# Other work dealt to the pairs of a scan by a budget of PE time, with a cap on ScalarE's parts between exps

## The chip, the cores and the metric

The kernel runs on one core of one Trainium2 chip. The metric is the time of the whole program on the device in microseconds; the time before is the median of three runs. A core has TensorE (PE in the profile), VectorE (DVE), ScalarE (ACT), GpSimd (POOL) and SyncE (SP), which here only issues the transfers. Each engine works through its own instructions in order, and semaphores tie the engines together.

## The reference: what is computed

The input is 8 sequences of 1024 tokens with 512 features, f32. It is normalized, and two branches read the result; the output is their sum with the input:

```python
xn = _layernorm(x)
x = x + mamba(xn, ...) + ffn(xn, w_gate, w_up, w_down)
```

The first branch is a Mamba block with 1024 inner channels and 16 states for each of them:

```python
x_branch, z = split(xn @ W_in)
xc = silu(causal_conv4(x_branch) + conv_b)
ssm = xc @ W_x                       # B (16), C (16) and one step value per token
dt = softplus(ssm[..., -1:] + dt_bias)
h = h * exp(dt * A) + (dt * xc) * B  # for every token in turn
y = (sum over states of h * C + xc * D_param) * silu(z)
out = y @ W_out
```

The second is a gated feed-forward layer of width 1408 in which inputs, weights and the hidden values are rounded to FP4 with one scale for each 16 values:

```python
h = silu(q(xn) @ q(w_gate).T) * (q(xn) @ q(w_up).T)
ffn = q(h) @ q(w_down).T
```

## The kernel before, in words

**Chunks and pairs.** The 8192 tokens are 16 chunks of 512. The scan over tokens is done for 128 rows at once, a row being one channel and one state: 32 channels by 4 states. A chunk has 8 channel blocks of 128 (j), 4 groups of states (q) and, for each, 4 sets of 32 channels that are worked on two at a time (h). So a chunk is 8 x 4 x 2 = 64 **pairs**, the whole kernel 1024. A pair is, in order of its dependencies: `make_u` (POOL, L471) multiplies dt*x by B; `make_a` (ScalarE, L480) makes two exps of 128x512 into PSUM; `scan` (DVE) runs two scans (L491), keeps the last state (L497) and multiplies by C (L499) into one of four `hc` buffers. Every second pair, `sum_states` (PE, L510) adds the states up into `py`. u is made two pairs ahead (three buffers), the exps one pair ahead (two PSUM buffers).

**Two sweeps.** `run` first prepares: weights and inputs are quantized, transposed and written to HBM, and the first chunk is projected. Then `sweep` goes over pairs 0 to 639 (chunks 0 to 9), and again over pairs 640 to 1023 (chunks 10 to 15). Each sweep spreads other work over its pairs:

- `finish` (L547), the output projection of the chunk before, in pairs 2 to 9 of a chunk (`END_Y`, `QUIET`).
- `ahead` (L447), the projections of the next chunk: for each of 8 blocks two halves of x (PE L331, then on ScalarE and DVE the convolution, L338 and L343), and z (PE L354, copied on ScalarE L361). Then `silus`, `parameters` (L381) and `steps_of` (softplus on ScalarE, L427). It runs from pair 9 on and is to be done by pair 43.
- in the first sweep `gate_up` (L564): 96 pieces, one for each chunk and 256 columns of the hidden width. A piece is four groups of matmuls (L589; gate for two pairs of token tiles, then up for the same), silu on ScalarE (L600), a multiply on DVE (L604), the scales on DVE (L613 to L619), five quantizing operations on POOL and ScalarE (L623 to L627, L55, L56), and `put`, which transposes on PE (L639), copies on ScalarE (L642) and stores.
- in the second sweep `downs` (L688): for each of 64 token tiles 11 matmuls (L705), whose sum `add` (L537) adds to the residual.

All are generators that yield the PE time (us) of the part that they have just issued. The order is written out by this planner, and the scheduler keeps it. At each pair, `sweep` issues the pair, then `issue` issues what has come due, and then takes parts from the generators. `later(n, work)` puts what follows a matmul (an evacuation, say) n pairs later. Gate/up's rate is its whole cost divided by the number of pairs that it may use, whatever else PE is given in that pair:

```python
slots = len(now) * (per - QUIET + END_Y) / per - TAIL
...
while spent < cost * passed / slots and self.room("other") and not self.hold:
```

**Banks.** Three PSUM banks serve all these matmuls. `bank` takes the next; `room` says whether the third last one has had the instruction issued that reads it out.

**Queues.** All transfers in the sweeps are issued by SP, in order. Projection weights (`weights`, L319) have two buffers; x's for the next block are asked for after the second half of x, z's at the block's start. The residual tile `r` (L543) is asked for after the matmuls that are added to it.

Of the kernel before, what the change touches and what calls it, by code (L numbers as in the profile page):

```python
# [17 lines left out]
P = 128  # L18
# [3 lines left out]
DOWN = 1.0 - 2.0**-23  # L22
STEEP = 0.47 * math.log(2.0)
# [10 lines left out]
QUIET = 9  # L34
TAIL = 12
# [47 lines left out]
class Net:  # L83
# [185 lines left out]
    def later(self, n, work, bank=None):  # L269

        self.due.setdefault(self.now + n, []).append((work, bank))
        if not self.timed:
            self.issue()

    def issue(self):
        while self.due.get(self.now):
            work, bank = self.due[self.now].pop(0)
            work()
            if bank is not None:
                bank[1] = False  # L280
        self.due.pop(self.now, None)
        if not self.timed and self.due:
            self.now = min(self.due)
            self.issue()
# [34 lines left out]
    def weights(self, s, j, off, name):  # L319
        w = self.pool.tile([P, self.KM, P], F32, tag="w", name=f"w{name}_{s.c}_{j}")  # L320
        self.nc.sync.dma_start(w, self.Win_v[:, :, off + j * P : off + (j + 1) * P])
        return w

    def project_x(self, s, j, i, w):
# [22 lines left out]
        self.later(1, convolve, b)  # L347

    def project_z(self, s, j, w):
# [13 lines left out]
        self.later(1, copy, b)  # L363

    def silus(self, s, h):
# [13 lines left out]
        self.later(1, store)  # L379

    def parameters(self, s):  # L381
# [24 lines left out]
        self.later(1, store, b)  # L406
        self.later(2, row)
        for h in range(self.J // 2):
            self.later(4 + 2 * h, lambda h=h: self.steps_of(s, h))
# [11 lines left out]
    def steps_of(self, s, h):  # L421
# [15 lines left out]
        self.later(1, rest)  # L437
# [99 lines left out]
    def add(self, t, b):  # L537
# [4 lines left out]
        r = self.pool.tile([P, self.DM], F32, tag="r", name=f"r_{t}_{seen}")  # L542
        nc.sync.dma_start(r, self.r_d[t] if seen else self.x[tok, :])  # L543
        self.later(1, lambda: nc.vector.tensor_tensor(r, r, b[0], ALU.add), b)
        self.later(2, lambda: nc.sync.dma_start(self.out[tok, :] if seen else self.r_d[t], r))

    def finish(self, s):  # L547
        nc = self.nc
        for i in range(self.TT):
            t = s.c * self.TT + i  # L550
            b = self.bank([P, self.DM], f"po_{t}")
# [7 lines left out]
            self.add(t, b)  # L559
# [4 lines left out]
    def gate_up(self, fp, chunks):  # L564
# [5 lines left out]
        full = []  # L570
# [35 lines left out]
        def scales(c, n, h, pu):  # L606
# [311 lines left out]
```

## Time and profile before

| what | value |
|---|---|
| median of 3 runs (lowest, highest) | 5607.41 us (5598.88, 5613.46) |
| the profiled execution, time and span | 5612.34 us, 5610.6 us |
| granted clock of PE over the span | 0.907 |
| first scan; first scan of the second sweep | 529.9 us; 3871.2 us |
| mean time of a pair, first and second sweep | 5.22 us, 4.44 us |
| two scans, one product with C | 2 x 1.227 to 1.287 us, 1.221 us |
| two exps; one u | 2 x 0.691 us; 2.360 us |

Durations are means of groups of the profiled execution. Busy time is what an engine spends on instructions of its own; waits and issues of transfers are not in it. A wait is written as the engine with the instruction that waited, an arrow, what released it, then the sum in us, the number of times and the longest. A busy PE is not a PE at its peak, since its clock can be granted in part (PEclk).

### The profile page before, as it was taken

How to read it: one execution, taken by the hardware profiler on the slowest of the kernel's cores; microseconds unless marked ns; L12 is line 12 of the kernel's file. 1: busy time of each engine (PE TensorE's matmuls, PEld its weight loads, DVE VectorE, ACT ScalarE, POOL GpSimd, SP SyncE). 2: the span in 40 equal slices, each digit the busy share in tenths (PEclk: the TensorE clock that was granted, in tenths of full speed). 3: DMA queues.
4: the chain of work that ended last, by engine and by line, in shares of the span. 5: the costliest groups of instructions: out<-in, count | busy, mean ns of one | idle time of the engine just before them, and what ended most of it. 6: DMA issues, size and time to landing. Idle time of an engine off the chain costs nothing.

```text
span 5610.6 us, 55655 instructions
## 1 busy us (share of the span) xinstructions
PE 4593.5 (82%) x17604; PEld 2572.4 (46%) x17604; DVE 4954.0 (88%) x5958; ACT 3022.8 (54%) x4042; POOL 3576.4 (64%) x1706
## 2 busy tenths in 40 slices
PE   4533888988898898988888798886989898989886
PEld 3322555645555465555555555552424242424221
DVE  5676889898988989999898898988999999999997
ACT  4664565655656566565655656554444444444432
POOL 6565676686766768676765867666465646465654
PEclk8755999989999998999999998997999999999997
DMA  6565565565665657566565655656676767676752
GB/s 175 156 184 152 136 172 153 160 193 147 180 161 152 166 154 188 151 184 167 159 174 154 182 153 166 168 153 178 171 198 176 196 174 196 176 198 172 194 144 69
DMA packets 635574, 937.75 MB, mean 167 GB/s; under 512 B 58624, under 2 KB 378112, under 8 KB 635152
## 3 DMA queue, kind: packets, MB, share of 16 engines
q1 hardware_dynamic: 624880, 931.66, 60.3%
q10 hardware_dynamic: 10400, 2.52, 0.2%
q8 instruction: 141, 2.31, 0.2%
q14 instruction: 153, 1.25, 0.1%
HBM read 676.81 MB, written 257.20 MB: 166 GB/s over the span
## 4 chain that ended last, share of the span: by engine, by line
DVE 42%; PE 24%; ACT 12%; issue 8%; DMA 7%; POOL 5%; SPq 1%; ACTq 0%; DVEq 0%; POOLq 0%
DVE ah L491 24%; DVE hc L499 7%; PE pu L589 4%; PE pz L354 4%; PE px L331 3%; ACT ah L480 3%; PE po L553 3%; DVE xc L343 3%; PE pod L705 3%; PE pg L589 2%; PE py L510 2%; DVE pu L613 2%; DMA rep<-ddd 1%; ACT L480 1%; DVE h L604 1%
## 5 line engine op out<-in xcount | busy, mean ns | idle before, releaser
L471 POOL TENSOR_TENSOR u<-rep,B 128x1024 f32<-128x1024 f32 x1024 | 2416.5, 2360 | 1504.7 <-DVE ah L491 1425.4
L480 ACT ACTIVATE ah<-rep,A 128x512 f32<-128x512 f32 x2048 | 1414.0, 691 | 1866.0 <-DVE hc L499 1818.4
L491 DVE TENSOR_TENSOR_SCAN ah<-ah,state,u 128x512 f32<-128x512 f32 x1024 | 1318.1, 1287 | 53.4 <-ACT ah L480 34.5
L491 DVE TENSOR_TENSOR_SCAN ah<-ah,u 128x512 f32<-128x512 f32 x1024 | 1256.7, 1227 | 89.5 <-ACT ah L480 67.7
L499 DVE TENSOR_TENSOR hc<-ah,C 128x1024 f32<-128x1024 f32 x1024 | 1250.0, 1221 | 56.7 <-PE py L510 16.5
L510 PE MATMUL py<-hc,summed 128*32 128x512 f32 x4096 | 713.8, 640 | 248.3 <-DVE hc L499 248.1
L589 PE MATMUL pu<-wu,xq 128*128 128x256 f32 (+1 forms) x3072 | 698.0, 385 | 62.8 <-ACT h L600 19.2
L589 PE MATMUL pg<-wg,xq 128*128 128x256 f32 (+1 forms) x3072 | 658.8, 370 | 45.5 <-DMA xq<-xqT 15.5
L705 PE MATMUL pod<-dT,hTr 128*128 128x512 f32 x1408 | 669.2, 624 | 14.9 <-DMA hTr<-hT 10.2
L589 PEld LDWEIGHTS pu<-wu,xq 128*128 128x128 f32 x3072 | 579.8, 205 | 194.6 <-ACT hT L642 25.7
L589 PEld LDWEIGHTS pg<-wg,xq 128*128 128x128 f32 x3072 | 548.7, 194 | 196.5 <-issue 78.0
L331 PE MATMUL px<-xT,wx 128*128 128x259 f32 x2048 | 547.9, 417 | 104.1 <-issue 24.1
L331 PEld LDWEIGHTS px<-xT,wx 128*128 128x128 f32 x2048 | 407.7, 206 | 284.9 <-issue 93.9
L354 PE MATMUL pz<-xT,wz 128*128 128x512 f32 x1024 | 479.7, 612 | 27.6 <-ACT ah L480 12.8
L343 DVE SCALAR_TENSOR_TENSOR xc<-px,cw,xc 128x256 f32<-128x256 f32 x768 | 369.6, 481 | 115.6 <-ACT xc L338 98.2
L553 PE MATMUL po<-Wout,y 128*128 128x512 f32 x1024 | 462.4, 603 | 1.2 <-DVE y L531 1.2
L705 PEld LDWEIGHTS pod<-dT,hTr 128*128 128x128 f32 x1408 | 272.6, 200 | 412.9 <-issue 391.6
L510 PEld LDWEIGHTS py<-hc,summed 128*32 128x32 f32 x4096 | 100.6, 111 | 669.8 <-DVE hc L499 404.0
L354 PEld LDWEIGHTS pz<-xT,wz 128*128 128x128 f32 x1024 | 193.5, 194 | 270.1 <-issue 207.4
L553 PEld LDWEIGHTS po<-Wout,y 128*128 128x128 f32 x1024 | 190.9, 191 | 267.7 <-issue 262.5
L623 POOL TENSOR_TENSOR qv<-h,rs 128x1024 f32<-128x1024 f32 x96 | 171.6, 1788 | 221.4 <-DVE rs L619 202.3
L480 ACT ACT_TABLE_LOAD x201 | 257.9, 1283 | 3.6
(108 smaller groups left out, 4182.9 us busy)
## 6 DMA issues: line engine op xcount, KB each, us to landing
rep<-ddd SPq DMA_DIRECT2D x512, 512.0 KB, 7.3
ddd<-dd SPq DMA_DIRECT2D x128, 512.0 KB, 3.2
hTr<-hT SPq DMA_DIRECT2D x64, 704.0 KB, 6.9
wg<-gu SPq DMA_DIRECT2D x80, 512.0 KB, 6.5
wu<-gu SPq DMA_DIRECT2D x80, 512.0 KB, 5.2
hT<-hT SPq DMA_DIRECT2D x80, 512.0 KB, 5.5
wx<-in_L_attn_W_in_dram SPq DMA_DIRECT2D x128, 256.0 KB, 3.5
wz<-in_L_attn_W_in_dram SPq DMA_DIRECT2D x128, 256.0 KB, 3.6
```

The costliest lines, as they stand in the source:

```text
L331: nc.tensor.matmul(px[:, : H0 + TH], w[:, k, :], s.xT[:, k, i * TH : i * TH + H0 + TH], start=(k == 0), stop=(k == self.KM - 1),)
L343: nc.vector.scalar_tensor_tensor(ca, px[:, k : k + TH], self.cw[:, j, k : k + 1], ca, ALU.mult, ALU.add)
L354: nc.tensor.matmul(b[0], w[:, k, :], s.xT[:, k, self.H0 :], start=(k == 0), stop=(k == self.KM - 1))
L471: self.nc.gpsimd.tensor_tensor(u, s.reps[j][:, h : h + 2, 1, :], s.B[q].unsqueeze(1).to_broadcast([P, 2, T]), ALU.mult)
L480: self.nc.scalar.activation(ah[:, i, :], s.reps[j][:, h + i, 0, :], AF.Exp, scale=self.A[:, g, q : q + 1])
L491: nc.vector.tensor_tensor_scan(ah[:, i, :], ah[:, i, :], u[:, i, :], 0.0 if s.first else self.state[:, g + i, q : q + 1], ALU.mult, ALU.add,)
L499: nc.vector.tensor_tensor(hc, ah, s.C[q].unsqueeze(1).to_broadcast([P, 2, T]), ALU.mult)
L510: nc.tensor.matmul(s.py[i * D4 : (i + 1) * D4, :], self.summed, hcs[i // 2][:, i % 2, :], start=False, stop=(q == NG - 1),)
L553: nc.tensor.matmul(b[0], s.y[:, j, i * P : (i + 1) * P], self.Wout[:, j, :], start=(j == 0), stop=(j == self.J - 1),)
L589: nc.tensor.matmul(b[0][:, i, :], xq[pair][:, k, i * P : (i + 1) * P], w[:, k, :], start=(k == 0), stop=(k == self.KM - 1),)
L623: self.later(1, lambda: tt(blocks(v), blocks(flat), spread(rs, blk), ALU.mult))
L705: nc.tensor.matmul(b[0], h[:, k, :], dT[:, k, :], start=(k == 0), stop=(k == self.KF - 1))
```

## The change

Seven things change together.

1. `sweep` keeps one budget for PE: the cost of the sweep's other work, of `finish` and `ahead` (29 and 68 us a chunk) and of the state sums, divided by the pairs. Each pair adds its share to a credit (at most 6 us), and parts are taken, of whichever generator is next in turn, until the credit is used.
2. `issue` stops issuing ScalarE's deferred parts in a pair once 2.0 us of them have been issued (`ENOUGH`); the rest is kept for the next pair. Parts carry a key ("a" for projections, "g" for gate/up, the tile's number for residuals), and what has the key of a kept part is kept too, so that their order stays. The last argument of `later` is ScalarE's time.
3. Both silus of a piece are one part, softplus follows at every third pair in place of every second, and `silus` of the projections three pairs later in place of two.
4. Projection weights have three buffers and are asked for further ahead; `finish` and `ahead` are each started once early (an initial `yield 0.0`) so that first loads are under way.
5. `r` is asked for before the matmuls that are added to it.
6. h is quantized in place, in three buffers (one h and two qv before). A piece may not begin before the third last piece has been handed to `put`.
7. The scale of h is written to SBUF at once (its copy, L616, is gone), and the factor that makes the reciprocal a little smaller is applied before it.

```diff
@@ -20,6 +20,7 @@
...
 DOWN = 1.0 - 2.0**-23
+UP = 1.0 + 2.0**-23
 STEEP = 0.47 * math.log(2.0)
...
@@ -32,6 +33,8 @@
...
 QUIET = 9
+ENOUGH = 2.0
+MOST = 6.0
 TAIL = 12
@@ -266,19 +269,29 @@
-    def later(self, n, work, bank=None):
-        self.due.setdefault(self.now + n, []).append((work, bank))
+    def later(self, n, work, bank=None, key=None, act=0.0):
+        self.due.setdefault(self.now + n, []).append((work, bank, key, act))
         if not self.timed:
...
     def issue(self):
+        used, kept = 0.0, []
         while self.due.get(self.now):
-            work, bank = self.due[self.now].pop(0)
+            item = work, bank, key, act = self.due[self.now].pop(0)
+            if key in [i[2] for i in kept] or (act and used >= ENOUGH and self.timed):
+                kept.append(item)
+                continue
+            used += act
             work()
-            if bank is not None:
-                bank[1] = False
+            for b in bank or ():
+                b[1] = False
         self.due.pop(self.now, None)
+        if kept:
+            self.due[self.now + 1] = kept + self.due.get(self.now + 1, [])
         if not self.timed and self.due:
...
@@ -317,7 +330,7 @@
...
     def weights(self, s, j, off, name):
-        w = self.pool.tile([P, self.KM, P], F32, tag="w", name=f"w{name}_{s.c}_{j}")
+        w = self.pool.tile([P, self.KM, P], F32, tag="w", name=f"w{name}_{s.c}_{j}", bufs=3)
         self.nc.sync.dma_start(w, self.Win_v[:, :, off + j * P : off + (j + 1) * P])
...
@@ -403,10 +416,10 @@
...
-        self.later(1, store, b)
-        self.later(2, row)
+        self.later(1, store, [b], "a", 0.6)
+        self.later(2, row, key="a")
         for h in range(self.J // 2):
-            self.later(4 + 2 * h, lambda h=h: self.steps_of(s, h))
+            self.later(4 + 3 * h, lambda h=h: self.steps_of(s, h), None, "a", 4.0)
...
@@ -446,19 +459,22 @@
...
-        w = self.weights(s, 0, 0, "x")
-        for h in range(self.J // 2):
-            for j in (2 * h, 2 * h + 1):
-                wz = self.weights(s, j, self.DI, "z")
-                for i in range(2):
-                    self.project_x(s, j, i, w)
-                    yield 2.0
-                if j + 1 < self.J:
-                    w = self.weights(s, j + 1, 0, "x")
-                self.project_z(s, j, wz)
-                if j % 2:
-                    self.later(2, lambda h=h: self.silus(s, h))
-                yield 3.5
+        ws = [self.weights(s, 0, 0, "x"), self.weights(s, 0, self.DI, "z"),
+              self.weights(s, 1, 0, "x")]
+        yield 0.0
+        for j in range(self.J):
+            for i in range(2):
+                self.project_x(s, j, i, ws[0])
+                if i and j + 1 < self.J:
+                    ws.append(self.weights(s, j + 1, self.DI, "z"))
+                yield 2.0
+            self.project_z(s, j, ws[1])
+            del ws[:2]
+            if j + 2 < self.J:
+                ws.append(self.weights(s, j + 2, 0, "x"))
+            if j % 2:
+                self.later(3, lambda h=j // 2: self.silus(s, h), None, "a", 4.7)
+            yield 3.5
         while s.active < self.J // 2:
...
@@ -534,20 +550,29 @@
-    def add(self, t, b):
+    def rest(self, pool, t):
+        seen = t in self.r_seen
+        r = pool.tile([P, self.DM], F32, tag="r", name=f"r_{t}_{seen}")
+        self.nc.sync.dma_start(r, self.r_d[t] if seen else self.x[t * P : (t + 1) * P, :])
+        return r
+    def add(self, t, r, b):
         nc = self.nc
...
         self.r_seen.add(t)
-        r = self.pool.tile([P, self.DM], F32, tag="r", name=f"r_{t}_{seen}")
-        nc.sync.dma_start(r, self.r_d[t] if seen else self.x[tok, :])
-        self.later(1, lambda: nc.vector.tensor_tensor(r, r, b[0], ALU.add), b)
-        self.later(2, lambda: nc.sync.dma_start(self.out[tok, :] if seen else self.r_d[t], r))
+        self.later(1, lambda: nc.vector.tensor_tensor(r, r, b[0], ALU.add), [b], t)
+        self.later(2, lambda: nc.sync.dma_start(self.out[tok, :] if seen else self.r_d[t], r), key=t)
...
         nc = self.nc
+        rs = [self.rest(self.pool, s.c * self.TT)]
+        yield 0.0
         for i in range(self.TT):
             t = s.c * self.TT + i
+            if i:
+                rs.append(self.rest(self.pool, t))
             b = self.bank([P, self.DM], f"po_{t}")
...
@@ -592,12 +617,12 @@
...
-        def silu(c, n, h, pair, b):
-            if pair == 0:
-                h.append(fp.tile(
-                    [P, self.TT, self.pieces[n][1]], F32, tag="h", name=f"h_{c}_{n}", bufs=1
-                ))
-            nc.scalar.activation(h[0][:, 2 * pair : 2 * pair + 2, :], b[0], AF.Silu)
+        def silus(c, n, h, pg):
+            h.append(fp.tile(
+                [P, self.TT, self.pieces[n][1]], F32, tag="h", name=f"h_{c}_{n}", bufs=3
+            ))
+            for pair in range(2):
+                nc.scalar.activation(h[0][:, 2 * pair : 2 * pair + 2, :], pg[pair][0], AF.Silu)
...
@@ -609,27 +634,27 @@
...
             flat = h[0].rearrange("p i f -> p (i f)")
-            top, sc_p = pu[:, 0, :blk], pu[:, 1, :blk]
+            top, up = pu[:, 0, :blk], pu[:, 1, :blk]
             nc.vector.tensor_reduce(top, blocks(flat), AX.X, ALU.max, apply_absolute_value=True)
-            nc.vector.tensor_scalar(sc_p, top, 1.0 / 6.0, TINY, ALU.mult, ALU.max)
             sc = fp.tile([P, blk], F32, tag="sc", name=f"sc_{c}_{n}")
-            nc.vector.tensor_copy(sc, sc_p)
-            nc.vector.reciprocal(top, sc_p)
+            nc.vector.tensor_scalar(sc, top, 1.0 / 6.0, TINY, ALU.mult, ALU.max)
+            nc.vector.tensor_scalar(up, sc, UP, None, ALU.mult)
             rs = fp.tile([P, blk], F32, tag="rs", name=f"rs_{c}_{n}")
-            nc.vector.tensor_scalar(rs, top, DOWN, None, ALU.mult)
-            v = fp.tile([P, K], F32, tag="qv", name=f"qv_{c}_{n}")
+            nc.vector.reciprocal(rs, up)
+            v = flat
             m = []
             tt = nc.gpsimd.tensor_tensor
-            self.later(1, lambda: tt(blocks(v), blocks(flat), spread(rs, blk), ALU.mult))
-            self.later(2, lambda: m.append(step_of(nc, fp, v, K, self.steep, f"{c}_{n}")))
-            self.later(3, lambda: tt(v, v, m[0], ALU.add))
-            self.later(4, lambda: tt(v, v, m[0], ALU.subtract))
-            self.later(5, lambda: tt(blocks(v), blocks(v), spread(sc, blk), ALU.mult))
-            self.later(5, lambda: full.append((c, n, v)))
+            self.later(1, lambda: tt(blocks(v), blocks(flat), spread(rs, blk), ALU.mult), key="g")
+            self.later(2, lambda: m.append(step_of(nc, fp, v, K, self.steep, f"{c}_{n}")), None, "g", 2.1)
+            self.later(3, lambda: tt(v, v, m[0], ALU.add), key="g")
+            self.later(4, lambda: tt(v, v, m[0], ALU.subtract), key="g")
+            self.later(5, lambda: tt(blocks(v), blocks(v), spread(sc, blk), ALU.mult), key="g")
+            self.later(5, lambda: full.append((c, n, v)), key="g")
...
             hv = hq.rearrange("p (i f) -> p i f", f=width)
+            stored.append(n)
             st = fp.tile([P, FB // P, T], F32, tag="hT", name=f"hT_{c}_{n}", bufs=1)
...
@@ -639,17 +664,22 @@
...
                     )
-                self.later(1, lambda d=d, b=b: nc.scalar.copy(st[:, d, :], b[0]), b)
+                self.later(1, lambda d=d, b=b: nc.scalar.copy(st[:, d, :], b[0]), [b], "g", 0.6)
                 if d == nb - 1:
...
                         self.hT_d[c][:, k0 : k0 + nb, :], st[:, :nb, :]
-                    ))
+                    ), key="g")
                 yield 0.6
...
         for i, (c, n) in enumerate(order):
+            while i - len(stored) == 3:
+                if full:
+                    yield from put(*full.pop(0))
+                else:
+                    yield 0.0
             load(c, n, 1)
...
@@ -659,10 +689,9 @@
...
                 if pair:
-                    for p in range(2):
-                        self.later(
-                            1, lambda c=c, n=n, h=h, p=p, b=pg[p]: silu(c, n, h, p, b), pg[p]
-                        )
+                    self.later(
+                        1, lambda c=c, n=n, h=h, pg=pg: silus(c, n, h, pg), pg, "g", 3.8
+                    )
                 yield 3.6 * self.pieces[n][1] / FB
...
@@ -671,14 +700,16 @@
...
                 if pair == 0:
-                    self.later(1, lambda h=h, b=b: times(h, 0, b), b)
+                    self.later(1, lambda h=h, b=b: times(h, 0, b), [b], "g")
                 else:
-                    self.later(1, lambda h=h, b=b: times(h, 1, b))
-                    self.later(1, lambda c=c, n=n, h=h, b=b: scales(c, n, h, b[0]), b)
+                    self.later(1, lambda h=h, b=b: times(h, 1, b), None, "g")
+                    self.later(1, lambda c=c, n=n, h=h, b=b: scales(c, n, h, b[0]), [b], "g")
                 if n == len(self.pieces) - 1 and i + 1 < len(order):
...
             del loads[:2]
+            if full and n == len(self.pieces) - 1:
+                yield from put(*full.pop(0))
         while full or self.due:
...
@@ -777,9 +809,13 @@
...
         per = len(pairs) // self.n
-        slots = len(now) * (per - QUIET + END_Y) / per - TAIL
-        spent = passed = 0.0
+        sums = NG * self.J * 1.1 + self.J * 0.9
+        left = cost + len(now) // per * (29.0 + 68.0 + sums)
+        slots = len(now) - TAIL
+        credit = 0.0
         for g in now:
...
@@ -787,7 +823,8 @@
...
                     self.step[c + 1] = self.begin(c + 1)
-                ends = self.finish(self.step[c - 1]) if c else iter(())
+                ends = self.finish(self.step[c - 1]) if c else iter([0.0])
+                next(ends)
                 nexts = self.ahead(self.step[c + 1]) if c + 1 < self.n else iter(())
...
@@ -797,38 +834,50 @@
...
             self.issue()
-            if h == 0 and g:
+            done = left
+            credit = min(credit + max(left, 0.0) / max(slots, 1), MOST)
+            slots -= 1
+            summed = h == 0 and g
+            if summed:
                 pc, pj, pq, _ = pairs[g - 1]
-            if h == 0 and g and pq == NG - 1:
-                self.sum_states(self.step[pc], pj, pq)
-            if self.hold or "other" in self.partly:
-                spent += next(others)
+                left -= 1.1 if pq else 2.0
+                if pq == NG - 1:
+                    self.sum_states(self.step[pc], pj, pq)
+            if k == QUIET - 5 and c + 1 < self.n:
+                next(nexts)
             if k == QUIET:
                 assert next(ends, None) is None
-            if END_Y <= k < QUIET:
-                while ended < 29.0 * (k - END_Y + 1) / (QUIET - END_Y) and self.room(
-                    "finish"
-                ):
-                    ended += next(ends, 1e9)
-            else:
-                passed += 1
-                while k >= QUIET and self.room("ahead") and (
-                    put < 68.0 * (k - QUIET + 1) / (PROJECTED - QUIET)
-                ):
-                    d = next(nexts, 1e9)
+            due = 29.0 * (k - END_Y + 1) / (QUIET - END_Y) if END_Y <= k < QUIET and c else 0.0
+            while left > done - credit or ended < due:
+                if self.hold or "other" in self.partly:
+                    of, d = others, "other"
+                elif END_Y <= k < QUIET and c:
+                    of, d = ends, "finish"
+                elif k >= QUIET and put < 68.0 * (k - QUIET + 1) / (PROJECTED - QUIET):
+                    of, d = nexts, "ahead"
+                else:
+                    of, d = others, "other"
+                if not self.room(d):
+                    break
+                d = next(of, 0.0)
+                if of is ends:
+                    ended += d
+                if d == 0.0 and of is nexts:
+                    d = next(others, 0.0) if self.room("other") else 0.0
+                elif of is nexts:
                     put += d
-                    if d == 0.0:
-                        break
-                while spent < cost * passed / slots and self.room("other") and not self.hold:
-                    d = next(others, 1e9)
-                    spent += d
-                    if d == 0.0:
-                        break
-            if h == 0 and g and pq < NG - 1:
+                left -= d
+                if d == 0.0:
+                    break
+            credit -= done - left
+            if summed and pq < NG - 1:
                 self.sum_states(self.step[pc], pj, pq)
             self.now += 1
-        for _ in others:
+        more = True
+        while more:
+            if self.room("other"):
+                more = next(others, None) is not None
             self.advance()
...
```

More of the change, by code (lines that the diff above doesn't have):

```diff
@@ L345, in convolve @@
                 )
-        self.later(1, convolve, b)
+        self.later(1, convolve, [b], "a", 0.6)
     def project_z(self, s, j, w):
@@ L361, in copy @@
             nc.scalar.copy(s.z[h][:, i, :], b[0])
-        self.later(1, copy, b)
+        self.later(1, copy, [b], "a", 0.6)
     def silus(self, s, h):
@@ L378, in silus @@
         s.active += 1
-        self.later(1, store)
+        self.later(1, store, key="a")
     def parameters(self, s):
@@ L435, in rest @@
                 s.dd_d[j] = d
-        self.later(1, rest)
+        self.later(1, rest, key="a")
     def fetch(self, s, j, n):
@@ L558, in finish @@
                     yield from self.part("finish", 3.6)
-            self.add(t, b)
+            self.add(t, rs[i], b)
             yield 3.6
@@ L569, in gate_up @@
         loads = []
-        full = []
+        full, stored = [], []
         def load_x(c, pair):
@@ L702, in downs @@
             h = hs.pop(0)
+            r = self.rest(fp, t)
             b = self.bank([P, self.DM], f"pod_{t}")
@@ L709, in downs @@
                     yield from self.part("other", 3.6)
-            self.add(t, b)
+            self.add(t, r, b)
             yield 2.8
```

## The prediction

> **What bounds the kernel now.** I read the page first (busy shares, clock, chain), then which waits VectorE (DVE) has inside the first sweep, then the busy time of each engine by stage of a chunk.
>
> ```profile
> PE 4593.5 (82%) x17604; PEld 2572.4 (46%) x17604; DVE 4954.0 (88%) x5958; ACT 3022.8 (54%) x4042; POOL 3576.4 (64%) x1706
> ...
> PEclk8755999989999998999999998997999999999997
> DVE 42%; PE 24%; ACT 12%; issue 8%; DMA 7%; POOL 5%; SPq 1%; ACTq 0%; DVEq 0%; POOLq 0%
> ```
>
> DVE is busy 88% of the span and holds 42% of the chain; PE is at 82% and holds 24%. Neither is saturated and both are near it, so what counts is how they take turns. The waits of DVE between 560 and 3820 us:
>
> ```profile
> DVE ah L491 <- ACT ah L480: 98.4, 52, 21.3
> DVE xc L343 <- ACT xc L338: 74.0, 48, 5.8
> DVE h L604 <- PE pu L589: 63.2, 46, 6.6
> DVE hc L499 <- PE py L510: 16.5, 5, 8.2
> ```
>
> These four are 252 us; with the smaller rows (5.9, 4.3, 3.3, 2.6, 0.6, 0.5) it is 269 us. The first is an exp that came late; the second and third are results of matmuls that came late (the rows of ScalarE's waits name PE px and PE pz ahead of xc and z). Now the stages. A chunk is 64 pairs. From the start times of the scans I took, for chunks 1 to 9, the windows of pairs 9 to 44 (projections run) and 44 to 64 (they are done). Columns: window, its length, busy us of PE, PEld, DVE, ACT, POOL, then clock and DMA. Chunk 5 of each kind, then the sum of the nine windows of pairs 9 to 44 and that of pairs 44 to 64:
>
> ```profile
> 2255.90:2445.50 189.60, 175.27 (x790) 116.04 (x789) 176.38 (x202) 114.62 (x155) 120.56 (x57) 0.99 0.58 163
> sum 1762.70, PE 1590.06 PEld 1056.85 DVE 1570.23 ACT 1030.46 POOL 1075.73; mean PE 176.67 PEld 117.43 DVE 174.47 ACT 114.50 POOL 119.53
> ```
>
> ```profile
> 2445.50:2539.80 94.30, 73.84 (x316) 49.35 (x316) 86.71 (x85) 66.46 (x83) 83.63 (x43) 0.86 0.59 172
> 3781.80:3871.20 89.40, 49.35 (x212) 23.72 (x212) 81.63 (x77) 57.40 (x77) 76.45 (x40) 0.71 0.57 169
> sum 870.90, PE 638.39 PEld 419.53 DVE 779.49 ACT 576.57 POOL 735.59; mean PE 70.93 PEld 46.61 DVE 86.61 ACT 64.06 POOL 81.73
> ```
>
> Pairs 9 to 44 take 195.9 us a chunk (1762.7/9; 5.60 a pair) with PE at 90% and DVE at 89%: two full engines that wait for each other. In pairs 44 to 64 (without the last chunk, whose work has run out: 781.5/8 = 97.7 us, 4.88 a pair) DVE is at 89% and PE at 75%, and the clock granted to PE is about 0.86. So PE's load is uneven: too dense early, too thin late.
>
> **The change part by part.**
>
> *PE's share per pair.* Before, gate_up is paced by 1372.8/558 = 2.46 us for each pair outside pairs 2 to 9 (85.8 us by the code's own costs x 16 chunks; 640 x 57/64 - 12 pairs), whatever else PE has. With 68/34 = 2.0 of projections and 42.4/64 = 0.66 of state sums that asks 5.12 a pair in pairs 9 to 44 (the trace has 176.67/35 = 5.05) and 3.12 after. The new budget is (1372.8 + 10 x 139.4)/628 = 4.41 for everything. I counted the instructions of both programs between the scans that enclose them. Multiplies h by pu go from 11.4 to 8.25 a chunk in pairs 9 to 44 and from 6.9 to 10.0 in pairs 44 to 64: 1.55 pieces of 15.6 us, 24 us of PE, move. The scales (one reduce a piece) move 5.5 to 4.4 and 3.6 to 5.0.
>
> For DVE that is, early, 3.1 x 0.636 + 1.1 x 2.3 us = 4.5 us less (rows: h 636 ns, reduce 1139, its four small followers 220 to 522), late 5.2 more. With the removed copy (below) the load of pairs 9 to 44 becomes PE 176.7 - 24 = 153, DVE 174.5 - 4.5 - 1 = 169; of pairs 44 to 64 DVE 87.2 + 5.2 - 1.1 = 91.3, PE 62.4 + 24 = 86 at full clock (3.12 x 20, which took 73.7 at the low clock). POOL there rises by 3.3 quantizing operations of 1.88 us to 4.4 a pair, ScalarE by 7.5 us (copies, silus, qm, 2.5 table loads) to 3.6: both under DVE's 4.57.
>
> What does such a stage take? Now DVE's share is 0.89 in both. A stage with smaller parts around the scans is in this trace too: pairs 9 to 44 of the second sweep take 164.3 us with DVE at 157.4 (0.96). The new early stage has slack on PE but keeps the gate_up couplings: between 0.91 and 0.96, I take 0.94, nearer the second, because most of the four waits come from PE being late. 169/0.94 = 179.8: 16.1 us a chunk gained (10.2 to 19.9). Late stage: between 0.87 and 0.93, I take 0.915: 99.8, so 2.1 lost (7.2 to 0.5). Net 14.0 a chunk; for 9.5 chunks (the tenth has no late stage) 133 us, half of the 269 us that DVE waits.
>
> *ScalarE's cap.* A pair's exps (2 x 691 ns) start when the second last pair's products are done and must be ready two pairs (at least 7.7 us) later, so about 4.9 us of other work fit into one pair. With the rows' durations, the old order puts up to 11.2 us (exps included) into one pair and over 7.2 into 5% of them; the new one at most 7.2, and 6.1 at the 95th. That is what can remove most of the 98.4 us, but for its longest, 21.3, at the start: the first silu waits for the first weights, which still happens. The rest is in the 0.94. Here a rule speaks against the change. Ahead of it the row: the exps' table loads.
>
> ```profile
> L480 ACT ACT_TABLE_LOAD x201 | 257.9, 1283 | 3.6
> ```
>
> The Trainium skill (ScalarE: Activation LUTs, What ACT_TABLE_LOAD costs, and its rules for authors) says to group by table set and to budget some 2.66 us for each switch, 1283 ns of load and 1380 of drain. Cutting ScalarE's work into smaller parts makes 495 loads in the new program for 476: by the row 19 x 1.28 = 24 us, by the page 51 us. The trace has the 1283 but no drain: a load begins 0.02 us after the operation ahead of it ended (3781.71, 3781.73) and silu follows at 3783.02. I take 24; ScalarE idles a third of these stages, so none of it lies on the path; if that cover is gone it is 24 us whole.
>
> *The copy removed.* Scales lose L616, 96 x 0.22 us = 21 us of DVE; sc is now read from SBUF, the other small operations keep their shapes (I cost them the same, 0.1 us each either way). In the DVE sums above.
>
> *h in place, three buffers; a piece may not start until the third one before it is transposed.* Space is unchanged (one h and two qv before). The wait is PE's: queued behind the transposes are gate, projections and the state sums, and behind those DVE's products (four hc buffers, two pairs). The quantizing chain takes five pairs at least and a piece lasts about 6.5, so it seldom binds: 0 us; bound -10 to +20.
>
> *Loads.* Weights are asked for three parts ahead in place of one or two: PE px waits 17.1 us for wx in the sweep. r is asked for before its matmuls: DVE waits 5.9 us in the first sweep and 20.6 (12.0 + 8.6) in the second for r. All these go through SP's one queue, whose order changes little; a load that waits for its buffer holds rep behind it, as it does now. Gain 0 to 40; I take 15, all in the second sweep, since px's share is in the 0.94.
>
> *Second sweep.* DVE is at 96% in its early stage (4.51 of 4.70 a pair), so evening out gains at most 164.5 - 158/0.97 = 1.6 us a chunk there; about 1.8 tiles of 9.5 us move into the late stage, whose pairs (4.12, DVE 3.87) then have PE at 4.0: that loses about as much. Net 0, plus the 15 us of r.
>
> *Preparation (530 us) and the last 36 us* keep their instructions; the projections come one step later under the same chain: 0, bound -5 to +5.
>
> Sum against the profiled run: 5612.3 - 133 - 15 = 5464. That run lies 4.9 us over the median, so about 5460.
>
> **Rivals.** *The coupling goes altogether* (0.96 and 0.93, and all loads hidden): 19.4 x 9.5 + 30 = 214, 5393. For it: the second sweep's 0.96. Against: silus, scales and convolutions still run through PSUM's three banks.
>
> *The stall only moves.* The deferred parts hold a bank until they are issued. Replaying the planner's arithmetic, 70 pairs of the new order end with over 1 us of unspent credit and no free bank, 37 of them in pairs 44 to 60, where softplus and silu compete; the old order has 5. With 0.91 early and 0.87 late, 3.0 x 9.5 = 29 us are left: 5578.
>
> *Slower.* Same place, but each starved pair is followed by a burst of 8 to 9 us on PE, whose first matmul waits for the silus issued in that very pair: exps, load, silus, 1.42 + 1.28 + 1.12 = 3.8 us. The profile has that wait now: PE's transposes wait 108 us for ScalarE's silu in 24 cases, longest 12.3. The sums then stand behind the burst, and DVE's products wait for their buffers (the 16.5 us row would grow). If three quarters of the 70 pay it, it costs 200 us: 5460 + 200 = 5660. It decides from 148/70 = 2.1 us each. Against: two pairs of DVE work (8.8 us) cover PE's lag.
>
> **How the numbers follow.** Likeliest, 0.61: 5460, own range 5400 to 5530 (the ends of the two shares). Coupling gone, 0.13: 5393. Moves, 0.16: 5578, of which 0.06 within 0.3% of the median (17 us, about what a measurement of this kernel can tell from no change). Slower, 0.10: 5660. Faster 0.61 + 0.13 + 0.10 = 0.84. The range 5380 to 5600 leaves out the slower case and the far end of the second.
>
> **What would show it.** Right: pairs 9 to 44 near 5.15 us with PE near 4.4 busy; pairs 44 to 64 near 5.0 with the clock over 0.93; DVE's waits for exps under 45 us and for xc and pu together under 80. Wrong: PE's waits for ScalarE's silu well over 108 us, or DVE's products waiting for PE py over 60 us; pairs 44 to 64 over 5.3; or pairs 9 to 44 still at 5.5 with PE at 4.4, which would mean that PE's density was not what held DVE.

## The result and the profile after

The changed kernel takes 5530.07 us (median of 4 runs, 5518.98 to 5530.98) and the kernel before, on the same chip, 5610.43: a ratio of 0.9855 (95% interval 0.9835 to 0.9875), 80 us less. The prediction was 5460, a gain of 147. The profiled execution has a span of 5529.0 us, 81.6 less than before. This is its page, the same lines as before the change.

```profile
PE 4534.9 (82%) x17604; PEld 2553.7 (46%) x17604; DVE 4938.8 (89%) x5862; ACT 3040.5 (55%) x4061; POOL 3573.5 (65%) x1706
...
PEclk8755999999999999989999999997999999999986
...
DVE 42%; PE 31%; ACT 8%; issue 8%; DMA 6%; POOL 3%; SPq 1%; DVEq 0%; ACTq 0%; POOLq 0%
```

In the clock row, slices 5 to 27 (the first sweep) have one 8 where they had three; slice 28, in which that sweep ends, is a 7 in both. The chain has as much DVE as before; PE has risen from 24% to 31%, and ScalarE has fallen from 12% to 8%. What DVE waits for in the first sweep (530 to 3800 us):

```profile
DVE h L629 <- PE pu L614: 115.4, 46, 30.3
DVE xc L356 <- ACT xc L351: 40.2, 19, 8.7
DVE r_False L565 <- PE po L578: 31.8, 16, 5.3
DVE hc L515 <- PE py L526: 20.8, 11, 5.4
DVE y L547 <- PE po L578: 6.5, 9, 1.0
DVE ah L507 <- ACT ah L496: 17.2, 17, 1.7
```

The wait for exps is nearly gone (98.4 to 17.2) and the one for xc is almost halved. The multiply of h by pu waits longer than before (115 for 63). 30.3 of it is the very first multiply, which stands in the third pair until the first weights have landed and their matmuls are done; before, this start stood in the exps' row (21.3 of the 98.4). Without the start, exps went from 77 to 17 and pu from 63 to 85. A new row is the residual's add, which waits for the output projection (po).

Now the stages. The windows of chunks 1 to 9 are cut at the scans' starts as for the prediction; each line is the sum over nine windows. First pairs 0 to 9 of the kernel before, which the prediction did not look at:

```profile
sum 358.60, PE 349.22 PEld 151.16 DVE 342.41 ACT 148.68 POOL 273.02; mean PE 38.80 PEld 16.80 DVE 38.05 ACT 16.52 POOL 30.34
```

The changed kernel, pairs 0 to 9, 9 to 44 and 44 to 64:

```profile
sum 407.20, PE 382.06 PEld 193.25 DVE 341.15 ACT 174.25 POOL 291.01; mean PE 42.45 PEld 21.47 DVE 37.91 ACT 19.36 POOL 32.33
...
sum 1651.50, PE 1438.87 PEld 895.04 DVE 1519.81 ACT 958.79 POOL 995.47; mean PE 159.87 PEld 99.45 DVE 168.87 ACT 106.53 POOL 110.61
...
sum 871.40, PE 709.73 PEld 510.40 DVE 802.50 ACT 629.68 POOL 784.07; mean PE 78.86 PEld 56.71 DVE 89.17 ACT 69.96 POOL 87.12
```

Pairs 9 to 44 gained 111.2 us (1762.7 to 1651.5); pairs 44 to 64 are as they were (870.9 and 871.4); pairs 0 to 9 lost 48.6. With the other parts of the program, by the scans' start times: preparation -6.4, chunk 0 +8.8, chunks 1 to 9 -62.2, chunks 10 to 14 -26.4, the last chunk and the end +4.6. The sum is -81.6.

### The profile page after: what moved, and what is told of

The parts are those of the page before. It is cut to its first block, busy times and chain, and to the rows that moved or that the text cites. A ratio compares the mean times of both kernels' runs of the same rounds, so it can differ in the third digit from the quotient of the medians.

```text
span 5529.0 us, 55758 instructions
## 1 busy us (share of the span) xinstructions
PE 4534.9 (82%) x17604; PEld 2553.7 (46%) x17604; DVE 4938.8 (89%) x5862; ACT 3040.5 (55%) x4061; POOL 3573.5 (65%) x1706
## 4 chain that ended last, share of the span: by engine, by line
DVE 42%; PE 31%; ACT 8%; issue 8%; DMA 6%; POOL 3%; SPq 1%; DVEq 0%; ACTq 0%; POOLq 0%
DVE ah L507 24%; DVE hc L515 7%; PE pod L737 6%; PE pu L614 5%; PE po L578 5%; PE pg L614 5%; DVE xc L356 4%; PE py L526 3%; PE pz L367 3%; ACT ah L496 2%; PE px L344 2%; DMA rep<-ddd 2%; DVE pu L638 1%; DVE h L629 1%; ACT L496 1%
## 5 line engine op out<-in xcount | busy, mean ns | idle before, releaser
L507 DVE TENSOR_TENSOR_SCAN ah<-ah,state,u 128x512 f32<-128x512 f32 x1024 | 1313.8, 1283 | 26.0 <-ACT ah L496 7.7
L515 DVE TENSOR_TENSOR hc<-ah,C 128x1024 f32<-128x1024 f32 x1024 | 1249.6, 1220 | 62.1 <-PE py L526 20.8
L614 PE MATMUL pg<-wg,xq 128*128 128x256 f32 (+1 forms) x3072 | 679.5, 379 | 93.0 <-issue 22.5
L614 PE MATMUL pu<-wu,xq 128*128 128x256 f32 (+1 forms) x3072 | 683.9, 380 | 82.4 <-ACT hT L667 24.6
L526 PE MATMUL py<-hc,summed 128*32 128x512 f32 x4096 | 650.5, 633 | 118.9 <-DVE hc L515 118.8
L737 PE MATMUL pod<-dT,hTr 128*128 128x512 f32 x1408 | 646.0, 610 | 39.1 <-DMA hTr<-hT 13.3
L614 PEld LDWEIGHTS pg<-wg,xq 128*128 128x128 f32 x3072 | 565.4, 199 | 237.0 <-issue 73.6
L614 PEld LDWEIGHTS pu<-wu,xq 128*128 128x128 f32 x3072 | 566.8, 200 | 208.6 <-ACT hT L667 39.5
L367 PE MATMUL pz<-xT,wz 128*128 128x512 f32 x1024 | 507.2, 641 | 71.8 <-issue 21.4
L496 ACT ACT_TABLE_LOAD x217 | 278.4, 1283 | 3.8
L647 POOL TENSOR_TENSOR h<-h,rs 128x1024 f32<-128x1024 f32 x96 | 171.6, 1788 | 163.0 <-DVE rs L643 153.2
```

What stands on the lines that cost most here:

```text
L367: nc.tensor.matmul(b[0], w[:, k, :], s.xT[:, k, self.H0 :], start=(k == 0), stop=(k == self.KM - 1))
L496: self.nc.scalar.activation(ah[:, i, :], s.reps[j][:, h + i, 0, :], AF.Exp, scale=self.A[:, g, q : q + 1])
L507: nc.vector.tensor_tensor_scan(ah[:, i, :], ah[:, i, :], u[:, i, :], 0.0 if s.first else self.state[:, g + i, q : q + 1], ALU.mult, ALU.add,)
L515: nc.vector.tensor_tensor(hc, ah, s.C[q].unsqueeze(1).to_broadcast([P, 2, T]), ALU.mult)
L526: nc.tensor.matmul(s.py[i * D4 : (i + 1) * D4, :], self.summed, hcs[i // 2][:, i % 2, :], start=False, stop=(q == NG - 1),)
L614: nc.tensor.matmul(b[0][:, i, :], xq[pair][:, k, i * P : (i + 1) * P], w[:, k, :], start=(k == 0), stop=(k == self.KM - 1),)
```

## The experiments

Each is the changed kernel with one edit (the last has two). Ratios are to the kernel before, measured with the run; the changed kernel has 0.9855 (0.9835 to 0.9875). A ratio of 0.001 is 5.6 us. A starved pair is one that in the planner's own arithmetic, not in the trace, ends with over 1 us of PE's credit unspent and no free bank.

### The cap alone taken away, and weakened

```diff
-ENOUGH = 2.0
+ENOUGH = 99.0
```

> The changed kernel without the cap on ScalarE's parts (no limit in place of 2.0 us a pair). Theory: the cap holds PSUM banks and so starves PE in pairs 48 to 60 and piles work up at the chunk's edge; in the planned order the starved pairs fall from 70 to 5, so pairs 0 to 9 go back from 5.0 to about 4.5 us, and the time is 5480 to 5510. Rival: the cap is what keeps the exps on time; without it the wait of DVE for exps goes from 17 us back to 80 or 100, and the time is 5580 to 5620.

Measured: 5678.36 us, ratio 1.0108 (1.0089 to 1.0126): slower than before the change, 142 us over the changed kernel by the ratios. My theory fell, and the rival's mechanism is not it either: DVE waits for exps 41 us, not 80 to 100. The stages (pairs 0 to 9, 9 to 44, 44 to 64) take 398.7, 1677.4 and 975.8: the edge of the chunk is as slow as with the cap, and pairs 44 to 64, where softplus runs, lose 104. The waits of PE, then of DVE, in the first sweep of this run:

```profile
PE pth L664 <- ACT h L625: 155.1, 34, 11.0
...
DVE h L629 <- PE pu L614: 194.2, 69, 8.4
```

For PE this is the row of the kernel before, then of the changed one:

```profile
PE pth L639 <- ACT h L600: 108.0, 24, 12.3
...
PE pth L664 <- ACT h L625: 31.6, 12, 5.6
```

DVE's row is 85 us in the changed kernel when its start is left out, which stands in another row here. The longest of PE's waits, by the timeline of this run (start, duration, engine, line, operation; idle time and its releaser in brackets):

```profile
2551.78 0.60 PE L664 MATMUL pth<-ident,h 128*128 128x128 f32 x4
...
2555.44 1.28 ACT L440 ACT_TABLE_LOAD   x1
2556.74 1.33 ACT L440 ACTIVATE dd<-row,dtb 128x512 f32<-128x512 f32 x2
2558.09 1.28 ACT L58 ACT_TABLE_LOAD   x1
2559.38 1.06 ACT L58 ACTIVATE qm<-h 128x1024 bf16<-128x1024 f32 x1
2560.47 1.15 ACT L59 ACTIVATE qm<-qm,steep 128x1024 bf16<-128x1024 bf16 x1
2561.64 1.28 ACT L625 ACT_TABLE_LOAD   x1
2562.93 0.66 ACT L625 ACTIVATE h<-pg 128x256 f32<-128x256 f32 x2
2563.37 1.12 PE L664 MATMUL pth<-ident,h 128*128 128x128 f32 x4 [10.99 <-ACT h L625]
...
2564.28 5.24 PE L614 MATMUL pu<-wu,xq 128*128 128x128 f32 x32
...
2567.84 0.42 DVE L629 TENSOR_TENSOR h<-h,pu 128x256 f32<-128x256 f32 x1 [6.15 <-PE pu L614]
```

The planner had issued softplus, qm and silu in one pair, so it took gate's bank to be free in that pair and issued the transposes that need it, and behind them the up matmuls. ScalarE worked through softplus and qm first, with three table loads. PE stood 11 us in front of the transposes, and DVE stood 6 us in front of the multiply, with the next pair's scans behind it. With the cap, silu is kept back, `room` is false, and the planner issues none of this in that pair. The starved pair that I counted as a cost in the prediction is what spares both queues the wait.

A weaker cap says the same:

```diff
-ENOUGH = 2.0
+ENOUGH = 4.0
```

> The changed kernel with the cap on ScalarE's parts at 4.0 us a pair in place of 2.0. Theory (the cap works by keeping PE and DVE from queueing behind a silu that is late, since the planner then knows the bank is taken): half of it is lost, PE's transposes wait again for silu (32 us now, 155 without a cap), and the time is 5570 to 5640. Rival: 2.0 is tighter than needed; the starved pairs fall from 70 to 17 and the time is 5490 to 5525.

Measured: 5583.55 us, 0.9951 (0.9936 to 0.9965). The wait of PE's transposes for silu:

```profile
PE pth L664 <- ACT h L625: 77.0, 25, 7.3
```

The theory's case: they wait 77 us, and 54 us of the 80 are lost although only 17 pairs are starved in the planned order.

### The budget alone undone

The old loop of `sweep` (gate/up at one rate), started as the new generators need it:

```diff
-            while left > done - credit or ended < due:
...
+                while spent < cost * passed / slots and self.room("other") and not self.hold:
```

> The changed kernel with the old pacing of PE's work (gate/up at one rate, whatever else PE has), all else as changed. Theory: the budget gives the gain of pairs 9 to 44, which go back from 5.25 to about 5.55 us; with the cap's starvation still there the time is 5590 to 5630. Rival: the gain is from the cap, the loads and the removed copy; 5525 to 5550.

Measured: 5606.82 us, 0.9982 (0.9976 to 0.9989). The theory's case: everything else in the change, the cap too, is worth 10 us together. Pairs 0 to 9, 9 to 44 and 44 to 64 of this run:

```profile
sum 351.10, PE 344.18 PEld 150.51 DVE 339.21 ACT 148.67 POOL 270.39; mean PE 38.24 PEld 16.72 DVE 37.69 ACT 16.52 POOL 30.04
...
sum 1810.70, PE 1580.89 PEld 1046.64 DVE 1557.41 ACT 1037.16 POOL 1070.77; mean PE 175.65 PEld 116.29 DVE 173.05 ACT 115.24 POOL 118.97
...
sum 845.30, PE 647.76 PEld 445.49 DVE 776.30 ACT 585.94 POOL 742.38; mean PE 71.97 PEld 49.50 DVE 86.26 ACT 65.10 POOL 82.49
```

So the gain is the budget's and the cap's together: the rest with the cap alone gives 10 us (in its profile, an execution 8 us over the median, chunks 0 to 9 lose 26 us and chunks 10 to 14 gain 19), the rest with the budget alone costs 61, all of it gives 81. And the budget is also what slows pairs 0 to 9: with the old pacing they take 351. Not undone one by one were the two silus as one part and the later softplus, the third buffer of the weights, and h in place; what each of them gives under the budget stays open.

### Where PE's work lies within a chunk

Two ways of taking PE's work out of one place (around the chunk's edge, and in the first pairs), one of putting the residual's add off, and two of shifting shares:

```diff
+            share = 0.5 if k >= 60 or k < END_Y else 1.0
-            credit = min(credit + max(left, 0.0) / max(slots, 1), MOST)
+            credit = min(credit + share * max(left, 0.0) / max(slots, 1), MOST)
```

> The changed kernel with half the share of PE's budget in pairs 60 to 64 and 0 to 2 of a chunk, the rest spread over the others. Theory: PE comes to the output projection (pairs 2 to 9) with a backlog; with less dealt before it, pairs 0 to 9 go from 5.0 to about 4.6 us a pair and the time from about 5535 to 5500 to 5520. Rival: PE is the bound over the whole chunk, so that what is taken out there is paid in pairs 9 to 60: 5530 to 5545.

Measured: 5544.73 us, 0.9883 (0.9868 to 0.9899). Pairs 0 to 9, then 9 to 44:

```profile
sum 342.10, PE 338.08 PEld 148.06 DVE 327.07 ACT 155.99 POOL 255.32; mean PE 37.56 PEld 16.45 DVE 36.34 ACT 17.33 POOL 28.37
...
sum 1724.00, PE 1475.62 PEld 937.82 DVE 1533.95 ACT 978.88 POOL 1025.92; mean PE 163.96 PEld 104.20 DVE 170.44 ACT 108.76 POOL 113.99
```

The work dealt around the edge is the cause of the slow edge: with half of it pairs 0 to 9 are faster than before the change (342 for 359). But the 65 us gained there are more than paid elsewhere, 72 us in pairs 9 to 44 and 40 in 44 to 64 (911.6); chunk 0, 22 us shorter, gives back a part. The rival's case.

Gate/up's first matmuls eight pairs later in the first chunk, with their loads under way:

```diff
         load(*order[0], 0)
+        for _ in range(8):
+            yield 0.0
```

> The changed kernel with gate/up's first matmuls eight pairs later (their loads are issued in pair 0). Theory: the 30 us that DVE waits in the first pairs is the first weights' landing plus a queue of four groups of matmuls; it goes, and what is put off costs 35 us of PE spread over 600 pairs: 5500 to 5515. Rival: PE is the bound, so that what is put off is paid in full: 5525 to 5540.

Measured: 5548.2 us, 0.9873 (0.9857 to 0.9889), not told from the changed kernel. Chunk 0 falls from 358.0 to 323.4 us, and chunks 1 to 9 rise from 2930.0 to 2964.8: what is put off is paid in full. Again the rival.

The add of the residual two pairs after its matmuls:

```diff
-        self.later(1, lambda: nc.vector.tensor_tensor(r, r, b[0], ALU.add), [b], t)
+        self.later(2, lambda: nc.vector.tensor_tensor(r, r, b[0], ALU.add), [b], t)
```

> The changed kernel with the residual's add two pairs after its matmuls in place of one. Theory: in pairs 2 to 9 DVE waits 3.6 us a chunk for the output projection because PE comes there with a backlog; with the add one pair later the 32 us of this wait go and the time is 5495 to 5512. Rival: PE itself is what these pairs wait for, so the wait moves to the products or to the multiplies of the next pairs; 5522 to 5535.

Measured: 5539.64 us, 0.9855 (0.9839 to 0.9872): no change. The waits of DVE in its first sweep show where this one went:

```profile
DVE hc L515 <- PE py L526: 44.8, 18, 5.4
...
DVE y L547 <- PE po L578: 18.8, 9, 2.6
```

From 20.8 and 6.5: the state sums stand behind the projection on PE, and DVE runs out of buffers for its products. In these pairs PE itself is waited for. But the equal total hides two parts: by the scans' starts chunks 0 to 9 are 8 us shorter, and chunks 10 to 14, whose residuals the edit puts off too, take 1441 us for 1419. No run puts off the first sweep's adds alone.

Shares after DVE's own load, and the other way:

```diff
+            share = 1.05 if QUIET <= k < 44 else 0.9
...
+            share = 0.95 if QUIET <= k < 44 else 1.08
```

> The changed kernel with PE's share of a pair at 1.05 in pairs 9 to 44 and 0.9 elsewhere, after DVE's own load (4.8 and 4.4 us a pair). Theory: equal PE time is not the best where DVE's time is unequal; 5505 to 5525. Rival: the early pairs are the ones in which PE and DVE hinder each other, and a denser PE there costs more than it gives: 5540 to 5565.

> The changed kernel with PE's share of a pair at 0.95 in pairs 9 to 44 and 1.08 elsewhere, the other way from the run with 1.05 and 0.9, which was 48 us slower than the changed kernel. Theory (where projections run, PE and DVE hinder each other most, and PE time is dearest there): pairs 9 to 44 fall from 5.25 to about 5.1 us, 5505 to 5525. Rival (equal shares are near the best, and what is moved meets the output projection in pairs 0 to 9): 5530 to 5560.

Measured: 5578.8 us, 0.9942 (0.9929 to 0.9955), and 5580.02 us, 0.9936 (0.9922 to 0.995). They are 49 and 45 us slower than the changed kernel by the ratios: the direction of both rivals, but more than either's range. By the scans' starts the first has pairs 9 to 44 at 5.38 us for 5.24; the second has them at 5.26, no better, and pairs 0 to 9 at 5.43 for 5.03. Equal PE time is the best of the three that were tried.

### Two small parts undone

The copy of the scale put back (96 x 0.22 us on DVE), and r asked for after its matmuls:

```diff
-            nc.vector.tensor_scalar(sc, top, 1.0 / 6.0, TINY, ALU.mult, ALU.max)
+            nc.vector.tensor_scalar(up, top, 1.0 / 6.0, TINY, ALU.mult, ALU.max)
+            nc.vector.tensor_copy(sc, up)
```

```diff
-    def add(self, t, r, b):
+    def add(self, t, pool, b):
+        r = self.rest(pool, t)
...
```

> The changed kernel with the copy of the scale put back (96 small instructions of 0.22 us on DVE). Theory: DVE is the bound in most pairs, and the 21 us come back whole: 5550 to 5560. Rival: they fall into DVE's waits: 5532 to 5542.

> The changed kernel with the residual tile asked for after its matmuls, as before. Theory (prediction's 15 us): DVE's waits for r in the second sweep come back, from 11 to over 20 us, and the time is 5540 to 5552. Rival: they are taken up by slack elsewhere: 5525 to 5538.

Measured: 5535.99 us, 0.9868 (0.985 to 0.9886), and 5539.76 us, 0.9862 (0.9843 to 0.988). Neither is told from the changed kernel. The copy's 21 us of DVE cost some 7 by the ratios, the rival's side; the two intervals leave room for anything from nothing to the whole 21. Of r, the second sweep's pairs take 4.50 us for 4.44: chunks 10 to 14 take 1440 us for 1419, while the profiles of the ten other runs that ask for r and add it as the changed kernel does have 1415 to 1430. So these 21 us are outside that spread. The first sweep is 13 us shorter in the same profile (chunks 0 to 9), for which no run shows a reason, and in the measured times I can't tell the whole from nothing.

### The multiply one pair later

If a wait that stands in an in-order queue is dearer than a bank that is planned as taken, DVE's longest wait should be worth a pair of delay:

```diff
-                    self.later(1, lambda h=h, b=b: times(h, 0, b), [b], "g")
+                    self.later(2, lambda h=h, b=b: times(h, 0, b), [b], "g")
...
-                    self.later(1, lambda h=h, b=b: times(h, 1, b), None, "g")
-                    self.later(1, lambda c=c, n=n, h=h, b=b: scales(c, n, h, b[0]), [b], "g")
+                    self.later(2, lambda h=h, b=b: times(h, 1, b), None, "g")
+                    self.later(2, lambda c=c, n=n, h=h, b=b: scales(c, n, h, b[0]), [b], "g")
```

> The changed kernel with DVE's multiply of h by the up product, and the scales behind it, two pairs after the matmuls in place of one. Theory (a wait that stands in DVE's queue is dearer than a bank held one pair longer): DVE's wait for PE pu, 115 us, falls under 50 and the time is 5480 to 5515. Rival: PE runs out of banks (92 starved pairs in the planned order for 70) and the wait goes over to PE: 5535 to 5570.

Measured: 5475.28 us, 0.9752 (0.9735 to 0.9768). This is the fastest version, 58 us under the changed kernel by the ratios: the theory's case, a little past its range. Its waits of DVE, and its pairs 9 to 44:

```profile
DVE ah L507 <- ACT ah L496: 69.8, 31, 27.4
DVE r_False L565 <- PE po L578: 46.2, 15, 8.7
DVE hc L515 <- PE py L526: 28.2, 13, 5.5
DVE xc L356 <- ACT xc L351: 26.9, 23, 2.7
DVE h L629 <- PE pu L614: 13.4, 10, 4.2
```

```profile
sum 1601.20, PE 1405.81 PEld 875.21 DVE 1512.98 ACT 951.71 POOL 981.02; mean PE 156.20 PEld 97.25 DVE 168.11 ACT 105.75 POOL 109.00
```

The wait for pu falls from 115 to 13. Of that, the start (27.4 here) has only gone over to the exps' row; without it pu falls from 85 to 13, and exps rise from 17 to 42. The planned order has 92 starved pairs for 70, and still it is faster. Pairs 9 to 44 gain another 50 us, with DVE at 0.945 of their time.

The same for the convolution, on top of it (ScalarE's part after one pair, DVE's after two, the bank free then):

```diff
-        self.later(1, convolve, [b], "a", 0.6)
+        self.later(1, scale, None, "a", 0.6)
+        self.later(2, convolve, [b], "a")
...
```

> As the run with the multiply and the scales two pairs after the up matmuls, and the convolution's part on DVE also one pair after ScalarE's part in place of the same pair. Theory (the same trade holds for the projections): DVE's wait for xc, 27 us, falls under 10 and the time is 5450 to 5470. Rival: banks are scarcer where projections run, PE is starved there and the time is 5475 to 5510.

Measured: 5503.58 us, 0.9809 (0.9792 to 0.9826), 32 us slower than without it by the ratios. Its waits of DVE, then of PE:

```profile
DVE hc L519 <- PE py L530: 67.3, 32, 8.9
...
DVE xc L359 <- ACT xc L351: 10.3, 8, 2.3
...
PE pz L371 <- ACT ah L500: 67.5, 20, 7.1
PE pth L668 <- POOL h L655: 37.1, 10, 13.1
```

The wait for xc does fall, 26.9 to 10.3, and others take its place: PE is late with the state sums (67 for 28) and waits itself for ScalarE and POOL (67.5 and 37.1 for 13.7 and 18.7). The rival's side. The planned order has 133 starved pairs for 92, so the three banks are short in the planner's arithmetic; that this is what costs the time is argued, not shown: no run has a fourth.

## Why the prediction was right, and where it was not

**The unevenness and the budget** were right. 24 us of PE a chunk were to leave pairs 9 to 44 for PE 153 and DVE 169; the windows have 159.9 (at a granted clock of 0.94 for 0.97) and 168.9. The old pacing puts pairs 9 to 44 to 1811 us, past the 1763 of before, and the clock granted in pairs 44 to 64 rises from 0.86 to 0.93 (means of chunks 1 to 8). Chunk 5's line of these pairs, with the clock behind the busy times:

```profile
2421.50:2520.30 98.80, 81.45 (x414) 60.93 (x413) 91.37 (x94) 72.19 (x92) 90.08 (x46) 0.91 0.67 195
```

**The share that DVE gets** was a size off. I took 0.94 for pairs 9 to 44 and it is 1519.8/1651.5 = 0.92: 12.4 us a chunk gained for 16.1. What held it back is the row that I had put among those that would shrink, DVE's wait for pu: xc and pu together were to come under 80 us and have 156. The multiply one pair later gives 0.945. For pairs 44 to 64, without the last chunk, the loss of 1.25 us a chunk is near the 2.1 predicted.

**The step that failed** is one that the sum does not name: pairs 0 to 9 were taken as unchanged. They lost 5.4 us a chunk, 49 us of the 111 gained. The new budget runs gate/up up to the chunk's edge and over it, and PE reaches the output projection, which has its own due time in pairs 2 to 9, with work still before it (PE busy 42.5 us a chunk for 38.8). The run with less work there shows that this is the cause, and also that it could not simply be moved. In two runs, this one and the one with the first chunk's start put off, PE's work that is taken out of one place is paid in another. So DVE's load over a share, which was my sum for the first sweep, does not set the time of a stage by itself; where PE's work is paid has to stand in it. Chunk 0, which the sum has among those that gain 14 us, lost 8.8; 6.5 of that is DVE's wait at the start (30.3 for 23.8).

**The cap** was right as a part of the gain and wrong in its reason. I gave it the exps' 98 us, and the banks that it holds I gave to a rival ("the stall only moves") and to the slower case. The exps' wait did fall to 17 us, but without the cap it is only 41, while the time is 142 us longer: what the cap saves, by the rows of three caps, is PE's and DVE's standing behind a late silu. In the slower case's terms, PE's transposes waiting for silu went from 108 down to 32, where it needed them well over 108. The count that these two rested on was off: of the 70 starved pairs 44 lie in pairs 44 to 60; 37 is the number in pairs 48 to 60.

**The second sweep** gained 26.4 us in chunks 10 to 14 for the 15 predicted from r. With r late, r's own row comes back (DVE waits 12.5 us for r_True's transfer for 6.8) and 21 us in one profile; so r's loads are near their term, and the rest is not settled. **Table loads** don't decide: all loads rose from 476 to 495 and the exps' from 201 to 217, at 1283 ns each; the old pacing has the same 495 and nearly the time of before, and the run without a cap, with the fewest (463), is the slowest. What the 19 more cost by themselves no run shows. **Preparation** came out 6.4 us shorter, past the bound of 5; the first scan lies between 523.1 and 532.7 us in these runs, so I leave it at that.

## What to carry to other kernels

On engines that work in order, a planner that leaves a pair empty because a bank is taken can be faster than one that fills it and lets the queue stand: count the waits by who stands in which queue, not only the empty slots. Let an evacuation be issued late enough that its matmul is done, as long as the buffers last; one pair here was worth 58 us on one consumer and cost 32 on the next. When work is evened out over a loop, look at the stage with its own due time (here the output projection) as well as the two stages between which it moves.

## What the runs showed of the hardware that I had not expected

A table load begins as soon as the operation before it has ended also in a run of three (softplus, qm and silu in 8.2 us, 2555.44 to 2563.6 above, 3 x 1.28 of it loads): the gaps ahead of the three loads are 0.01 to 0.02 us, and no drain shows in the timeline. And PE's granted clock was higher in the stages in which PE was busier: in pairs 44 to 64 without the last chunk 0.86 with PE busy 75% of the time before, and 0.93 with 85% (673.5 of 791.5 us) after; in pairs 9 to 44 0.97 with 90% before, and 0.94 with 87% after.
